# Ranks by stage for the first groups of a planned graph network kernel

## The chip, the core and the metric

The kernel runs on one core of one Trainium2 chip. The metric is the device time of one execution in microseconds (us); lower is better. A core has five engines that work side by side, each through its own instructions in a fixed order: PE (matrix products; its weight loads are shown apart as PEld), DVE and ACT (elementwise work), POOL (some small elementwise work here), and SP, which here only issues DMA transfers. They wait for each other through semaphores.

## The reference

128 graphs of 128 nodes with 256 features pass through three graph-attention layers and one gated graph network of three steps. Cut to what matters:

```python
# x [128, 128, 256], adj [128, 128, 128]
for W, a in three_layers:                    # attention layers
    h  = relu(layernorm(x))
    Wh = h @ W
    e  = leaky_relu((Wh @ a1)[:, :, None] + (Wh @ a2)[:, None, :], 0.2)
    p  = softmax(where(adj > 0, e, -9e15), axis=-1)
    x  = x + elu(p @ Wh)                     # the third layer also times nodemask
h = h0 = relu(layernorm(x))
A = adj != 0
for i in range(3):                           # gated steps
    aggr = A^T @ (h @ weight[i])
    r, z = sigmoid(aggr @ w_ih.T + h @ w_hh.T + biases)    # by halves
    n    = tanh(i_n + r * h_n)
    h    = (1 - z) * n + z * h
x = x + h
```

All of it is in 32-bit floats.

## The kernel before

**Tiling.** The graphs are cut into 33 groups: group 0 and group 32 hold 2 graphs, the others 4 (SIZES). A group g goes through seven stages: attention layers 0, 1, 2 and the normalisation behind them (`gat`, `attention`, stages l = 0 to 3), then the gated steps i = 0, 1, 2 (`gru`, `step`), and last the residual and the store (`end`).

In an attention layer, the statistics of x (st, ve, rs, nm), the normalised xn (ACT) and the scores (scr, e on DVE) are followed by a row of scores for every node. In groups 0 and 1 ("near") PE makes that row (e2, L625; the trace shows its tile as e) and PE turns the softmax weights em into at (atp, L682). In the others ("far") both go through DRAM: de and er carry the scores (L616, L618), d_at and at the turned weights. Then PE forms ahp = weights times xn (L710), ACT copies it to ah (L717), PE forms hp = ah times W (L729), and ACT and DVE add elu(hp) into x (t L743, x L745 and L747). Behind layer 2 the normalised state is hn (L778); its turned form h comes from PE (hTp, L793) in group 0 and through d_h and h in DRAM in the others, and a DVE copy (L858) puts it into the steps' layout.

A step aggregates (agp, L978; copied to ag), forms the gates' products in a recursive two by two scheme with seven products instead of eight (a, e, b from L952 and nn, nnb from L939, each for h and for ag, with DVE's sums t13 and t24 of halves), then the candidate ni (L1034), tanh, and mixes the new state. Between the steps the state is turned for the next agp: by PE (hnp, L839) in the near groups and in the last ones, through DRAM (d_hn, hn) in the others.

Before all that stands the setup: the attention vectors (`attention_weights`: ab, vp, va), the node mask (`mask`), the turned and combined weights of the gated network (`hidden`, `transposed`, `combined`: tiles whh, wih, gt, wcp, wcn, with combinations on POOL) and the biases. The steps of groups 0 and 1 wait for the whole setup (`after = last_setup`).

**What sets the order.** Nothing runs when the code above it is called: each operation is added to a `Plan` with its engine, a cost written by hand, a rank (a wish for its place; small is early) and what it reads and writes. `Plan.issue` (L108) then puts all operations in one order. Each turn it finds for each engine the operation that could start first by its costs; among those that could start within WINDOW of that one it takes the lowest rank. Operations whose rank is more than AHEAD above the lowest unfinished rank are held back. The order within each engine is fixed there, when the program is built; on the chip only the waits remain.

The ranks come from a few constants: an attention layer l of group g has rank 3g minus LEADS[g] plus 2.25 l, the normalisation behind it 5.5 instead of 2.25 l (`attention` L582, `gat` L755 and L770); step i of group g starts at BASES[g] + GAPS[g] i for the first four groups and at 3g + 2i for the others (`start`, L1167). The operations of a step have ranks near that start. The setup of the gated network has one rank, SETUP = -4.0 (L280); the attention vectors have 1.5 l - 8.0 (L299) and their loads l - 11.2. The loads of a group's x and adj have the rank of its layer 0 less 4 and less 3.6.

Of the kernel before, what the change touches and what calls it, by code (L numbers as in the profile page):

```python
# [14 lines left out]
P = 128  # L15
# [24 lines left out]
class Plan:  # L40
# [67 lines left out]
    def issue(self):  # L108
# [77 lines left out]
def kernel(  # L186
# [25 lines left out]
    nc = tc.nc  # L212
# [53 lines left out]
    def act(cols):  # L266
        return 0.25 + cols / 1400
# [70 lines left out]
    def mask():  # L338
        nm = val(su, "nm", [N], "nm")
        nmp = bank("gat", "nmp")  # L340
        load(64, SETUP, lambda: nc.sync.dma_start(nm.t[:B], nodemask), writes=[nm])
        add("PE", 0.11, SETUP, lambda: nc.tensor.transpose(nmp.t[:, :B], nm.t[:B], ident[:B, :B]),
            reads=[nm], writes=[nmp])
        add("ACT", act(P), SETUP, lambda: nc.scalar.copy(nmT.t, nmp.t[:, :B]),
            reads=[nmp], writes=[nmT])

    mask()
# [9 lines left out]
    def kept(ps, m, blocks, name):  # L357

        rz, n, raw = blocks

        def row(c):
            return ps.t.rearrange("p (g c o) -> p g c o", g=2, c=KD)[:, :, c, :]

        add("ACT", act(2 * D), SETUP, lambda: nc.scalar.mul(
            raw.t[:, m, :], ps.t, 0.5), reads=[ps], writes=[(raw, m)])
        add("ACT", act(D), SETUP, lambda: nc.scalar.mul(
            rz.t[:, m, :].rearrange("p (g o) -> p g o", g=2), row(1), 0.5,
        ), reads=[ps], writes=[(rz, m)])

    def combinations(to, raw, gates):  # L370

        def low(k):
            return raw.t[:, k, :].rearrange("p (g c o) -> p g c o", g=gates, c=KD)[:, :, 0, :]

        def of(i):
            return to.t[:, i, :].rearrange("p (g o) -> p g o", g=gates)

        def both(i, a, b, op, reads):
            return add("POOL", pool(gates * P), SETUP, lambda: nc.gpsimd.tensor_tensor(
                of(i), a(), b(), op=op), reads=reads, writes=[(to, i)])  # L380

        return [
            both(4, lambda: low(0), lambda: low(1), OP.add, [raw]),
            both(6, lambda: of(0), lambda: low(0), OP.subtract, [(to, 0), raw]),
            both(5, lambda: of(4), lambda: of(0), OP.subtract, [(to, 4), (to, 0)]),
            both(2, lambda: of(1), lambda: of(5), OP.subtract, [(to, 1), (to, 5)]),
            add("POOL", pool(gates * P), SETUP, lambda: nc.gpsimd.tensor_scalar(
                of(3), low(1), -1.0, None, op0=OP.mult), reads=[raw], writes=[(to, 3)]),
        ]

    def loaded(src, name):
        rows = src.shape[0] // P
        ld = val(su, "wld", [O3 // P, D], f"{name}_ld")
        load(128 * rows, SETUP, lambda: nc.sync.dma_start(
            ld.t[:, :rows], src.rearrange("(r p) d -> p r d", p=P)), writes=[ld])
        return ld, rows

    def turned_rows(ps, ld, k, r0, n, takes):

        def turn(r):  # L400
            add("PE", 0.11, SETUP, lambda: nc.tensor.transpose(
                ps.t[:, r * P : (r + 1) * P], ld.t[:, r0 + r, k * P : (k + 1) * P], ident
            ), reads=[ld], writes=[(ps, r)], takes=takes)

        for r in range(n):
            turn(r)

    def transposed(src, dst, name):
        ld, rows = loaded(src, name)

        def part(k, r0, n):
            ps = bank("gru", f"{name}_{k}_{r0}")
            turned_rows(ps, ld, k, r0, n, [dst])
            add("ACT", act(n * P), SETUP, lambda: nc.scalar.copy(
                dst.t[:, k, r0 * P : (r0 + n) * P], ps.t[:, : n * P]
            ), reads=[ps], writes=[(dst, (k, r0))])

# [4 lines left out]
    def hidden():  # L422
# [5 lines left out]
        def part(k):  # L428
# [5 lines left out]
            add("ACT", act(D), SETUP, lambda: nc.scalar.mul(  # L434
                raw_n.t[:, k, :], pn.t[:, :D], 0.25), reads=[pn], writes=[(raw_n, k)])
            add("ACT", act(P), SETUP, lambda: nc.scalar.mul(
                n.t[:, k, :], pn.t[:, P : 2 * P], 0.25), reads=[pn], writes=[(n, k)])

        for k in range(KD):
            part(k)  # L440
        return blocks, combinations(rz, raw, 2) + combinations(n, raw_n, 1)

    WHH, last_setup = hidden()
    wih = val(su, "wih", [KD, O3], "wih", bufs=1)
    transposed(w_ih, wih, "wih")

    def combined(i):
        gt = val(su, "gt", [KD, D], f"gt_{i}")
        transposed(gweight[i], gt, f"gt{i}")
        blocks = blocks_of(f"wc_{i}")  # L450

        def product(ps, m, o0, n):
            def one(k):
                add("PE", pe(n), SETUP, lambda: nc.tensor.matmul(
                    ps.t[:, :n], gt.t[:, k, m * P : (m + 1) * P], wih.t[:, k, o0 : o0 + n],
                    start=(k == 0), stop=(k == KD - 1),
                ), reads=[gt, wih], writes=[ps], takes=blocks)
# [4 lines left out]
        def part(m):  # L462
# [5 lines left out]
            return add("ACT", act(D), SETUP, lambda: nc.scalar.mul(  # L468
                blocks[1].t[:, m, :], pn.t[:, :D], 0.5), reads=[pn], writes=[(blocks[1], m)])

        return blocks, [part(m) for m in range(KD)] + combinations(blocks[0], blocks[2], 2)
# [2 lines left out]
    for i in range(STEPS):  # L474
        blocks, ops = combined(i)
        WC.append(blocks)
        last_setup += ops

    bi, bh, brz = (const_val(n, [NCH]) for n in ("bi", "bh", "brz"))

    def load_bias(dst, src):
        def fn():
            with nc.allow_non_contiguous_dma(reason="768 biases, once"):
                nc.sync.dma_start(dst.t, src.rearrange("(c p) -> p c", p=P))
        load(4, SETUP, fn, more=3.0, writes=[dst])

    load_bias(bi, b_ih)
    load_bias(bh, b_hh)
    add("DVE", dve(8), SETUP, lambda: nc.vector.tensor_add(brz.t, bi.t, bh.t),
        reads=[bi, bh], writes=[brz])  # L490
    add("DVE", dve(8), SETUP, lambda: nc.vector.tensor_scalar_mul(brz.t, brz.t, 0.5),
        reads=[brz], writes=[brz])
    add("DVE", dve(8), SETUP, lambda: nc.vector.tensor_scalar_mul(bh.t, bh.t, 0.5),
        reads=[bh], writes=[bh])


# [718 lines left out]
```

## Time and profile before

| | us |
|---|---|
| three runs | 2604.84, 2606.74, 2608.95 |
| median | 2606.74 |
| the profiled execution | 2606.36 |
| its span, first to last instruction | 2604.6 |
| mean granted PE clock | 0.988 of full |

The profile is of one execution. Its page gives each engine's busy time, the span in forty slices of 65 us, the chain of work that ended last, and groups of instructions. Two more views of the same trace are used: tables by stage (busy time of each engine in a stretch of time, and the clock that PE was granted in it), and the timeline (one engine's instructions in order, merged where they are alike, with the idle time before them and what ended it in brackets). A matrix product of 32-bit floats shows as two records on PE, a transpose as one. Names in the trace leave out the groups' numbers.

### The profile page before, as it was taken

What the parts mean: (1) busy time and instruction counts of PE and PEld (TensorE: products, weight loads), DVE (VectorE), ACT (ScalarE), POOL (GpSimd) and SP (SyncE); (2) the same over time, 40 slices, a digit from 0 to 9 for tenths busy, and PEclk for the clock granted to TensorE, in tenths of its full rate; (3) what the DMA queues carried; (4) which work ended last, traced back from release to release, by engine and by line L of the source; (5) the groups of instructions that cost most, each with busy time, mean ns of one, the idle gap of its engine ahead of it and who ended that gap; (6) DMA issues with size and microseconds to landing.
All of it is one profiled execution on the core that took longest, in us unless ns stands there. A gap on an engine that the chain in (4) does not pass through costs nothing.

```text
span 2604.6 us, 39011 instructions
## 1 busy us (share of the span) xinstructions
PE 2535.1 (97%) x12549; PEld 2104.6 (81%) x12549; DVE 2105.3 (81%) x4955; ACT 1768.6 (68%) x4411; POOL 225.8 (9%) x328
## 2 busy tenths in 40 slices
PE   7699799999999999999999999999999999999998
PEld 5578688788888888888888888888888888888877
DVE  6577777888888888888888888888888888888765
ACT  6566666676777676677767677766767776766554
POOL 3100000000000000000000000000000000000000
PEclk8899899999999999999999999999999999999999
DMA  3122423434334333333443434433343343333320
GB/s 92 53 54 67 108 62 101 110 101 114 94 103 108 94 108 103 112 95 98 107 104 102 114 94 105 106 97 109 103 111 93 98 112 101 94 102 85 82 63 13
DMA packets 503123, 245.75 MB, mean 94 GB/s; under 512 B 280579, under 2 KB 472067, under 8 KB 502918
## 3 DMA queue, kind: packets, MB, share of 16 engines
q1 hardware_dynamic: 502918, 243.25, 35.0%
q8 instruction: 100, 1.64, 0.3%
q14 instruction: 105, 0.86, 0.1%
HBM read 139.28 MB, written 103.87 MB: 93 GB/s over the span
## 4 chain that ended last, share of the span: by engine, by line
PE 94%; DVE 3%; ACT 2%; DMA 0%; issue 0%; SPq 0%; POOL 0%; ACTq 0%; DVEq 0%; POOLq 0%
PE b L952 19%; PE hp L729 13%; PE ni L1034 12%; PE a L952 12%; PE e L952 12%; PE ahp L710 7%; PE agp L978 6%; PE nn L939 6%; PE nnb L939 5%; DVE scr L597 0%; DVE x L745 0%; DVE st L506 0%; DVE x L747 0%; PE hnp L839 0%; ACT em L653 0%
## 5 line engine op out<-in xcount | busy, mean ns | idle before, releaser
L1034 PE MATMUL ni<-ag,wc_n 128*128 128x512 f32 (+1 forms) x792 | 353.1, 583 | 4.1 <-DVE ni L1028 4.1
L729 PE MATMUL hp<-w,ah 128*128 128x256 f32 x1536 | 355.0, 384 | 1.2 <-ACT ah L717 1.2
L729 PEld LDWEIGHTS hp<-w,ah 128*128 128x128 f32 x1536 | 285.3, 191 | 61.6 <-ACT ah L717 15.2
L597 DVE SCALAR_TENSOR_TENSOR scr<-xn,va 128x256 f32<-128x256 f32 x732 | 269.8, 417 | 35.9 <-ACT xn L589 35.5
L1034 PEld LDWEIGHTS ni<-ag,wc_n 128*128 128x128 f32 x792 | 148.5, 192 | 130.8 <-issue 105.5
L978 PEld LDWEIGHTS agp<-am,hn 128*128 128x128 f32 x1536 | 206.2, 193 | 50.6 <-issue 30.4
L743 ACT ACTIVATE t<-hp 128x512 f32<-128x512 f32 x192 | 104.8, 594 | 208.7 <-PE hp L729 208.5
L1039 ACT ACTIVATE wn<-ni,bi 128x512 f32<-128x512 f32 (+1 forms) x198 | 133.5, 674 | 151.8 <-PE ni L1034 105.3
L978 PE MATMUL agp<-am,hn 128*128 128x128 f32 x1536 | 211.8, 277 | 10.8 <-ACT hn L778 7.5
L952 PE MATMUL a<-h,whh_rz 128*128 128x256 f32 (+1 forms) x792 | 209.5, 375 | 11.2 <-DVE h L858 10.1
L710 PEld LDWEIGHTS ahp<-at,xn 128*128 128x128 f32 x1536 | 192.7, 197 | 27.1 <-issue 20.4
L512 POOL TENSOR_SCALAR ve<-st 128x4 f32<-128x4 f32 (+1 forms) x132 | 28.5, 216 | 2117.1 <-DVE st L506 1822.7
L710 PE MATMUL ahp<-at,xn 128*128 128x128 f32 x1536 | 194.4, 281 | 9.2 <-DMA at<-d_at 7.2
L589 ACT ACTIVATE xn<-x,nm,rs 128x256 f32<-128x256 f32 x366 | 201.0, 594 | 1.8 <-DVE nm L518 1.8
L952 PE MATMUL a<-ag,wc_rz 128*128 128x256 f32 (+1 forms) x792 | 200.4, 374 | 0.0
L745 DVE SCALAR_TENSOR_TENSOR x<-hp,x 128x512 f32<-128x512 f32 x192 | 124.1, 686 | 93.8 <-ACT t L743 93.6
L506 DVE BATCH_NORM_STATS2 st<-x 128x6 f32<-128x512 f32 x256 | 171.2, 690 | 2.6 <-DMA x<-in_x_dram 2.4
L636 ACT ACTIVATE em<-er,e 128x128 f32<-128x128 f32 x366 | 163.7, 522 | 6.1 <-DMA er<-de 6.1
L952 PEld LDWEIGHTS a<-h,whh_rz 128*128 128x128 f32 x792 | 141.0, 191 | 27.2 <-DVE h L858 10.6
L653 ACT ACTIVATE em<-em,nmx 128x128 f32<-128x128 f32 x384 | 149.5, 392 | 11.3 <-DVE nmx L649 11.0
L952 PEld LDWEIGHTS a<-ag,wc_rz 128*128 128x128 f32 x792 | 141.1, 191 | 15.1 <-issue 0.5
L717 ACT COPY ah<-ahp 128x512 f32<-128x512 f32 (+1 forms) x198 | 113.3, 573 | 56.8 <-PE ahp L710 50.6
(158 smaller groups left out, 5574.2 us busy)
## 6 DMA issues: line engine op xcount, KB each, us to landing
d_hn<-tr_hn SPq DMA_DIRECT2D x116, 256.0 KB, 2.4
hn<-d_hn SPq DMA_DIRECT2D x464, 64.0 KB, 2.3
er<-de SPq DMA_DIRECT2D x90, 256.0 KB, 3.9
d_at<-tr_at SPq DMA_DIRECT2D x90, 256.0 KB, 2.0
at<-d_at SPq DMA_DIRECT2D x360, 64.0 KB, 2.1
x<-in_x_dram SPq DMA_DIRECT2D x31, 512.0 KB, 5.1
d_h<-tr_h SPq DMA_DIRECT2D x31, 512.0 KB, 2.8
h<-d_h SPq DMA_DIRECT2D x124, 128.0 KB, 2.8
```

Of the source, the lines that this page charges most:

```text
L506: add("DVE", dve(T), rank, lambda: nc.vector.bn_stats(st.t[:, b, :].rearrange("p b s -> p (b s)"), xt.t[:, b, :].rearrange("p b d -> p d b ...
L589: add("ACT", 0.45, rank, lambda: nc.scalar.activation(xn.t[:, b, :], xt.t[:, b, :], AF.Relu, bias=nm.t[:, b : b + 1], scale=rs.t[:, b : b ...
L597: add("DVE", dve(D), rank, lambda: nc.vector.scalar_tensor_tensor(scr.t, xn.t[:, b, :], 1.0 if far else rs.t[:, b : b + 1], VA[l].t[:, s, ...
L636: add("ACT", 0.55 if far else 0.42, rank, lambda: nc.scalar.activation(em.t[:, b, :], e2_row(b), AF.Prelu, bias=e.t[:, 0, b : b + 1], alph ...
L653: add("ACT", 0.42, rank, lambda: nc.scalar.activation(em.t[:, b, :], em.t[:, b, :], AF.Exp, bias=nmx.t[:, b : b + 1], accum_out=sm.t[:, b ...
L710: add("PE", pe(P), rank, lambda: nc.tensor.matmul(summed(ps, b), xn.t[:, b, k * P : (k + 1) * P], turned_weights(b), start=True, stop=True ...
L729: add("PE", pe(D), rank, lambda: nc.tensor.matmul(hp.t[:, b * D : (b + 1) * D], ah.t[:, k, c * P : (c + 1) * P], W[l].t[:, k, :], start=(k ...
L939: op = add("PE", pe(H), at, lambda: nc.tensor.matmul(ps.t[:, o : o + H], WHH[1].t[:, blk, :], rhs(), start=starts, stop=True, skip_group_c ...
L952: nc.tensor.matmul(ps.t[:, gate * D : gate * D + H], w[0].t[:, blk, gate * P : (gate + 1) * P], rhs(), start=go, stop=w is not WHH, skip_g ...
L978: nc.tensor.matmul(ps.t[:, b * P : (b + 1) * P], s, am.t[:, b, :], start=True, stop=True)
L1034: add("PE", pe(TG), rank + 0.45 + 0.05 * c, lambda k=k: nc.tensor.matmul(ni[c].t[:, :TG], WC[i][1].t[:, k, c * P : (c + 1) * P], ag.t[:, k ...
L1039: add("ACT", act(TG) + 0.05, quick, lambda: nc.scalar.activation(wn[c].t[:, :TG], ni[c].t[:, :TG], AF.Tanh, bias=bi.t[:, cn : cn + 1]), re ...
```

## The change

Only ranks and the constants that govern their use change; wherever an operation of the setup had SETUP, it now has setup_rank().

1. In the plan, WINDOW goes from 0.1 to 0.097 and AHEAD from 3.5 to 4.12; while the lowest unfinished rank is at most UNTIL = -1.46, EARLY = 5.0 stands for AHEAD.
2. The setup's one rank becomes a list by piece: the mask -4.77 instead of -4.0, all other pieces -3.63.
3. The attention vectors of the three layers get -6.42, -7.21, -4.35 instead of -8.0, -6.5, -5.0; their loads -11.17, -10.17, -7.80 instead of -11.2, -10.2, -9.2.
4. The first ten groups' ranks come from a table with a number for each stage (ATT) instead of a number for each group, and the steps' starts of the first eight groups from another (STARTS). Later groups keep the formula. Group 3's attention, for example, goes from 2.0, 4.25, 6.5, 7.5 to -0.38, 1.67, 4.29, 4.81; group 2's from -4.5, -2.25, 0, 1 to -3.70, -1.92, 1.59, 3.59; group 1's from -6.0, -3.75, -1.5, -0.5 to -7.16, -4.64, -3.85, -2.65; group 0's first step from 0 to 1.68.

```diff
-    WINDOW = 0.1
-    AHEAD = 3.5
+    WINDOW = 0.097
+    AHEAD = 4.12
+    EARLY = 5.00
+    UNTIL = -1.46
...
-            limit = by_rank[low].rank + self.AHEAD
+            limit = by_rank[low].rank
+            limit += self.AHEAD if limit > self.UNTIL else self.EARLY
...
-    SETUP = -4.0
+    SETUPS = [-4.77, -3.63, -3.63, -3.63, -3.63, -3.63, -3.63]
+    setting = [0]
+
+    def setup_rank():
+
+        return SETUPS[setting[0]]
...
-        rank = 1.5 * l - 8.0
+        rank = [-6.42, -7.21, -4.35][l]
...
-        first = l - 11.2
+        first = [-11.17, -10.17, -7.80][l]
...
+    setting[0] = 1
     WHH, last_setup = hidden()
+    setting[0] = 2
     wih = val(su, "wih", [KD, O3], "wih", bufs=1)
     transposed(w_ih, wih, "wih")
 
     def combined(i):
+        setting[0] = 3 + i
...
-        rank = 3.0 * g - lead(g) + SPAN * l
+        rank = stage(g, l)
...
-        rank = 3.0 * g - lead(g)
+        rank = stage(g, 0)
...
-        rank = 3.0 * g - lead(g) + HEAD
+        rank = stage(g, 3)
...
-    BASES = [0.00, 3.00, 6.00, 9.00]
-    GAPS = [2.00, 2.00, 2.25, 2.00]
...
-    LEADS = [7.50, 9.00, 10.50, 7.00, 7.75, 7.25, 8.50, 8.50, 8.50, 8.50]
...
+    ATT = [
+        [-8.90, -4.73, -3.23, -1.30],
+        [-7.16, -4.64, -3.85, -2.65],
+        [-3.70, -1.92, 1.59, 3.59],
+        [-0.38, 1.67, 4.29, 4.81],
+        [3.81, 5.72, 6.93, 8.03],
+        [7.96, 10.27, 13.26, 12.41],
+        [9.50, 11.75, 14.74, 15.00],
+        [12.46, 14.80, 17.00, 18.00],
+        [15.66, 17.97, 20.00, 21.29],
+        [18.50, 20.75, 23.00, 24.00],
+    ]
+    STARTS = [
+        [1.68, 2.28, 4.42],
+        [3.03, 4.63, 6.47],
+        [5.97, 6.79, 10.50],
+        [9.00, 11.18, 12.82],
+        [12.28, 14.00, 16.00],
+        [14.67, 16.85, 19.17],
+        [17.30, 19.87, 22.34],
+        [21.00, 23.00, 25.06],
+    ]
+
+    def stage(g, l):
+
+        return ATT[g][l] if g < len(ATT) else 3.0 * g - LEAD + (SPAN * l if l < 3 else HEAD)
 
     def start(g, i):
 
-        return BASES[g] + GAPS[g] * i if g < len(BASES) else 3.0 * g + 2.0 * i
+        return STARTS[g][i] if g < len(STARTS) else 3.0 * g + 2.0 * i
```

More of the change, by code (lines that the diff above doesn't have):

```diff
@@ L340, in mask @@
         nmp = bank("gat", "nmp")
-        load(64, SETUP, lambda: nc.sync.dma_start(nm.t[:B], nodemask), writes=[nm])
-        add("PE", 0.11, SETUP, lambda: nc.tensor.transpose(nmp.t[:, :B], nm.t[:B], ident[:B, :B]),
+        load(64, setup_rank(), lambda: nc.sync.dma_start(nm.t[:B], nodemask), writes=[nm])
+        add("PE", 0.11, setup_rank(), lambda: nc.tensor.transpose(nmp.t[:, :B], nm.t[:B], ident[:B, :B]),
             reads=[nm], writes=[nmp])
-        add("ACT", act(P), SETUP, lambda: nc.scalar.copy(nmT.t, nmp.t[:, :B]),
+        add("ACT", act(P), setup_rank(), lambda: nc.scalar.copy(nmT.t, nmp.t[:, :B]),
             reads=[nmp], writes=[nmT])
@@ L362, in row @@
             return ps.t.rearrange("p (g c o) -> p g c o", g=2, c=KD)[:, :, c, :]
-        add("ACT", act(2 * D), SETUP, lambda: nc.scalar.mul(
+        add("ACT", act(2 * D), setup_rank(), lambda: nc.scalar.mul(
             raw.t[:, m, :], ps.t, 0.5), reads=[ps], writes=[(raw, m)])
-        add("ACT", act(D), SETUP, lambda: nc.scalar.mul(
+        add("ACT", act(D), setup_rank(), lambda: nc.scalar.mul(
             rz.t[:, m, :].rearrange("p (g o) -> p g o", g=2), row(1), 0.5,
@@ L378, in both @@
         def both(i, a, b, op, reads):
-            return add("POOL", pool(gates * P), SETUP, lambda: nc.gpsimd.tensor_tensor(
+            return add("POOL", pool(gates * P), setup_rank(), lambda: nc.gpsimd.tensor_tensor(
                 of(i), a(), b(), op=op), reads=reads, writes=[(to, i)])
@@ L386, in combinations @@
             both(2, lambda: of(1), lambda: of(5), OP.subtract, [(to, 1), (to, 5)]),
-            add("POOL", pool(gates * P), SETUP, lambda: nc.gpsimd.tensor_scalar(
+            add("POOL", pool(gates * P), setup_rank(), lambda: nc.gpsimd.tensor_scalar(
                 of(3), low(1), -1.0, None, op0=OP.mult), reads=[raw], writes=[(to, 3)]),
@@ L393, in loaded @@
         ld = val(su, "wld", [O3 // P, D], f"{name}_ld")
-        load(128 * rows, SETUP, lambda: nc.sync.dma_start(
+        load(128 * rows, setup_rank(), lambda: nc.sync.dma_start(
             ld.t[:, :rows], src.rearrange("(r p) d -> p r d", p=P)), writes=[ld])
@@ L400, in turn @@
         def turn(r):
-            add("PE", 0.11, SETUP, lambda: nc.tensor.transpose(
+            add("PE", 0.11, setup_rank(), lambda: nc.tensor.transpose(
                 ps.t[:, r * P : (r + 1) * P], ld.t[:, r0 + r, k * P : (k + 1) * P], ident
@@ L413, in part @@
             turned_rows(ps, ld, k, r0, n, [dst])
-            add("ACT", act(n * P), SETUP, lambda: nc.scalar.copy(
+            add("ACT", act(n * P), setup_rank(), lambda: nc.scalar.copy(
                 dst.t[:, k, r0 * P : (r0 + n) * P], ps.t[:, : n * P]
@@ L433, in part @@
             turned_rows(pn, ld, k, 4, 2, [*blocks, raw_n])
-            add("ACT", act(D), SETUP, lambda: nc.scalar.mul(
+            add("ACT", act(D), setup_rank(), lambda: nc.scalar.mul(
                 raw_n.t[:, k, :], pn.t[:, :D], 0.25), reads=[pn], writes=[(raw_n, k)])
-            add("ACT", act(P), SETUP, lambda: nc.scalar.mul(
+            add("ACT", act(P), setup_rank(), lambda: nc.scalar.mul(
                 n.t[:, k, :], pn.t[:, P : 2 * P], 0.25), reads=[pn], writes=[(n, k)])
@@ L453, in one @@
             def one(k):
-                add("PE", pe(n), SETUP, lambda: nc.tensor.matmul(
+                add("PE", pe(n), setup_rank(), lambda: nc.tensor.matmul(
                     ps.t[:, :n], gt.t[:, k, m * P : (m + 1) * P], wih.t[:, k, o0 : o0 + n],
@@ L467, in part @@
             product(pn, m, 2 * D, D)
-            return add("ACT", act(D), SETUP, lambda: nc.scalar.mul(
+            return add("ACT", act(D), setup_rank(), lambda: nc.scalar.mul(
                 blocks[1].t[:, m, :], pn.t[:, :D], 0.5), reads=[pn], writes=[(blocks[1], m)])
@@ L477 @@
         last_setup += ops
+    setting[0] = 6
     bi, bh, brz = (const_val(n, [NCH]) for n in ("bi", "bh", "brz"))
@@ L484, in fn @@
                 nc.sync.dma_start(dst.t, src.rearrange("(c p) -> p c", p=P))
-        load(4, SETUP, fn, more=3.0, writes=[dst])
+        load(4, setup_rank(), fn, more=3.0, writes=[dst])
     load_bias(bi, b_ih)
     load_bias(bh, b_hh)
-    add("DVE", dve(8), SETUP, lambda: nc.vector.tensor_add(brz.t, bi.t, bh.t),
+    add("DVE", dve(8), setup_rank(), lambda: nc.vector.tensor_add(brz.t, bi.t, bh.t),
         reads=[bi, bh], writes=[brz])
-    add("DVE", dve(8), SETUP, lambda: nc.vector.tensor_scalar_mul(brz.t, brz.t, 0.5),
+    add("DVE", dve(8), setup_rank(), lambda: nc.vector.tensor_scalar_mul(brz.t, brz.t, 0.5),
         reads=[brz], writes=[brz])
-    add("DVE", dve(8), SETUP, lambda: nc.vector.tensor_scalar_mul(bh.t, bh.t, 0.5),
+    add("DVE", dve(8), setup_rank(), lambda: nc.vector.tensor_scalar_mul(bh.t, bh.t, 0.5),
         reads=[bh], writes=[bh])
@@ L1148, in gru @@
         return step, end
-    URGENT = 1.0
-    BASES = [0.00, 3.00, 6.00, 9.00]
-    GAPS = [2.00, 2.00, 2.25, 2.00]
+    URGENT = 1.00
     SPAN = 2.25
@@ L1160 @@
     LEAD = 8.5
-    LEADS = [7.50, 9.00, 10.50, 7.00, 7.75, 7.25, 8.50, 8.50, 8.50, 8.50]
-    def lead(g):
-        return LEADS[g] if g < len(LEADS) else LEAD
+    ATT = [
[22 more added lines that the diff above has]
+        return ATT[g][l] if g < len(ATT) else 3.0 * g - LEAD + (SPAN * l if l < 3 else HEAD)
     def start(g, i):
-        return BASES[g] + GAPS[g] * i if g < len(BASES) else 3.0 * g + 2.0 * i
+        return STARTS[g][i] if g < len(STARTS) else 3.0 * g + 2.0 * i
     work, h = {}, {}
```

## The prediction

> **What bounds the kernel now.** I read the page first: its busy shares, the forty slices, the chain that ended last.
>
> ```profile
> PE 2535.1 (97%) x12549; PEld 2104.6 (81%) x12549; DVE 2105.3 (81%) x4955; ACT 1768.6 (68%) x4411; POOL 225.8 (9%) x328
> ...
> PE   7699799999999999999999999999999999999998
> ...
> PEclk8899899999999999999999999999999999999999
> ...
> PE 94%; DVE 3%; ACT 2%; DMA 0%; issue 0%; SPq 0%; POOL 0%; ACTq 0%; DVEq 0%; POOLq 0%
> ```
>
> PE is full except in slices of the first 340 us, and there its clock is short as well. So the kernel has two regimes, and a new order can win only where PE has holes. The table by stage (columns: stretch, its length, busy time of PE, weight loads, DVE, ACT, POOL with counts, clock, DMA share, GB/s) says how much:
>
> ```profile
> 0.00:40.00 40.00, 32.16 (x140) 23.26 (x141) 25.82 (x91) 25.19 (x72) 10.00 (x22) 0.83 0.50 150
> 40.00:140.00 100.00, 69.60 (x331) 54.04 (x330) 54.90 (x156) 56.59 (x162) 22.45 (x31) 0.85 0.12 35
> 140.00:200.00 60.00, 56.84 (x349) 49.23 (x349) 48.49 (x140) 43.78 (x118) 7.97 (x11) 1.00 0.24 62
> 200.00:300.00 100.00, 98.61 (x491) 82.48 (x491) 77.14 (x187) 69.55 (x173) 5.72 (x8) 1.00 0.28 77
> 300.00:340.00 40.00, 25.12 (x106) 20.47 (x105) 29.16 (x76) 23.50 (x61) 4.20 (x7) 0.79 0.37 94
> 480.00:500.00 20.00, 16.09 (x77) 13.77 (x76) 15.72 (x43) 9.07 (x26) 1.86 (x4) 1.00 0.46 110
> 604.00:2500.00 1896.00, 1895.57 (x9309) 1578.25 (x9308) 1596.13 (x3684) 1319.07 (x3257) 152.62 (x217) 1.00 0.38 101
> ```
>
> From 604 to 2500 us PE idles 0.43 us: nothing is to be had. From 40 to 140 us no engine is full (PE 70%, DVE 55%, ACT 57%): serial chains bound it. PE's timeline shows the holes and who ended them:
>
> ```profile
> 62.89 0.47 PE L682 MATMUL atp<-ident,em 128*128 128x128 f32 x1 [5.54 <-ACT em L666]
> 84.56 0.47 PE L625 MATMUL e<-ident,e 128*128 128x128 f32 x1 [5.72 <-DVE scr L597]
> 117.23 3.65 PE L1034 MATMUL ni<-ag,wc_n 128*128 128x256 f32 x8 [3.31 <-DVE ni L1028]
> 128.09 3.75 PE L710 MATMUL ahp<-at,xn 128*128 128x128 f32 x16 [7.21 <-DMA at<-d_at]
> 310.40 2.27 PE L978 MATMUL agp<-am,hn 128*128 128x128 f32 x8 [7.48 <-ACT hn L778]
> 322.15 2.08 PE L952 MATMUL a<-h,whh_rz 128*128 128x256 f32 x4 [6.72 <-DVE h L858]
> 476.94 1.05 PE L978 MATMUL agp<-am,hn 128*128 128x128 f32 x8
> 487.56 1.13 PE L952 MATMUL a<-h,whh_rz 128*128 128x256 f32 x4 [3.37 <-DVE h L858]
> ```
>
> Now a measure that holds idle time and slow clock together. In the dense stretch a PE product (two records) follows the last after 0.223 us (128 columns), 0.432 (256) or 0.858 (512), a transpose after 0.11. Over all PE instructions that is 2493 us of full-clock work. "Lag" is time minus the full-clock work done by then; what a new order wins is lag. Before: 18 us at 40, 45 at 98 (group 0's first aggregation), 52 at 121 (its first GRU step done), 59 at 128, 70 at 200, 72 at 300, 90 at 322, 93 at 480, 97 at 500, 101 at 2520, 107.5 at PE's last instruction.
>
> **What the Trainium skill says.** "TensorE: Matmul & The Clock Gate", Part 1: an idle window of about 3.4 us halves PE's clock until it has been busy for about as long. The trace agrees: the granted clock from 309 to 323 us is 0.50, and the eight aggregation records take 2.27 us at 310 against 1.05 at 477. So the 14.9 us idle from 300 to 322 cost 17.6 us of lag. "Perfetto Trace Analysis", Optimization Strategy: regimes with different limits gain from being interleaved; the stage table shows two such. "DMA: Bandwidth & Descriptors", Latency and other measured facts: about 2 us fixed cost per transfer; the page's issues land in a median 2.0 to 2.8 us, and one turned state (out and back) is two of them.
>
> **The change part by part.** It adds and removes no instruction: in the built programs each engine has the same ones (6349 products and transposes on PE, 1659 DMAs on SP). Only the order differs, and only early: PE's is identical from the instruction that ran at 604 us, POOL's from 312, DVE's, ACT's and SP's from 762. So the tail costs as before, and AHEAD 4.12 and WINDOW 0.097 do nothing in the steady part. All that counts is the lag on entering the common order: 97 before. I count in the new order how much full-clock PE work ("cover") lies between a producer and its consumer on PE, and hold it against how long that hand-over took in the trace.
>
> *Start to group 0's first aggregation.* The long chain is group 1's three layers. Before, all products of the weights' setup (wcp and wcn, 12 of 0.858 and 12 of 0.432, 15.5 us) stood ahead of the second half of its layer 1's e2 rows, which ran at 56.8; the 5.5 us hole follows. Now two of the 24 do, and those rows end at 29 us of PE work instead of 38. The chain by the trace: hp of layer 0 done at 36; to e2 8.5 (36.5 to 45.0) plus 2 to issue; to atp 5.7; to ahp 1.9; ahp and ah 2.4, hp 3.5: 60. Layer 2: 9.9 to e2 (the 84.56 wait ended it), then 0.5, 5.7, 1.9, 2.4, 3.5: 84. Group 0's hTp follows its hp by 8.1, at about 86; group 2's ahp and hp take 5: first aggregation at 91 with 58.4 us of work done, lag 32 against 45. DVE and ACT bound this from the other side: the new order brings group 3's first layer in here, so at the end of group 0's first step they have done 81.5 and 80.9 us against 74.9 and 76.9. From 40 us DVE owes 55.7; at 55% (as now) that ends at 141, at 81% (as from 140 to 200) at 109. I take 77%: the step ends at 112 with 68.9 us of PE work, lag 43 against 52, keeping 36 (86%) and 61 (62%) for the range. A step needs 13 us (agp at 138.6 to ni at 151.5), so by the chain alone it ends at 107.
>
> *To 139 us of work.* The 7.21 us wait: cover from group 2's hp to its next ahp goes from 16.1 to 27.4, against 31.6 us that hand-over took; shortfall at most 4, mostly eaten by gaps in between. Interleaved with the steps of groups 0 and 1 remain short waits on agp and b (seven of 0.5 to 0.7 us from 138 to 184 before). +7: lag 50 against 70.
>
> *Groups 1 to 3.* Before +2 to 300 us; I take +3, since covers of 2.7 and 4.8 us before group 1's hnp are near the 3 us of tanh and mix (rows of 0.69). The hole of 17.6: cover from group 3's last hp to its agp goes from 3.4 to 48.1. Gone. Group 2's same hand-over shrinks from 37 to 21.5, but there what counts is its turned state: 11.9 us of work from its transpose to the h copy, against 9.2 (313.2 to 322.4) and 11.2 (476.6 to 487.8) measured. +0.5.
>
> *To the common order.* +3 to 480 as before. The 487.56 wait, 4.5 us of lag: group 5's normalised state is transposed 7.3 us of work after its hp instead of 13.4, leaving 11.4 for the turn that took 11.2. Group 4's state between steps 1 and 2 has only 9.5 us of cover instead of 23.9; such a turn took 11.8 without a wait at group 2. +2.5 for both (0 to 9).
>
> Sum: 43 + 7 + 3 + 0.5 + 3 + 2.5 = 59, against 97.3: 38 us less. POOL's and SP's reordering I cost at nothing: the combinations on POOL end by 44 us of work, 25 ahead of the first step's end, and x and adj of groups 4 to 9 are loaded 80 us of work or more before use. If that cover failed, a step would show a DMA wait. The profiled execution took 2606.36 (span 2604.6 and 1.8 around it), 0.4 below the median 2606.74: forecast 2568.
>
> **The rivals.**
> - Denser packing (17%). DVE and ACT reach 86% early, as DVE's 95% from 140 to 160 suggests they can: lag 36 + 5 + 2 + 3 = 46, 51 us less, 2555. Against: each engine takes its queue in the plan's order, and the near layers are serial.
> - The vector engines become the early bound (14%). At 62% the first step ends at 130, lag 61 + 16 = 77, 20 us less, 2586. For: the ranks now put group 3's exchanges among the near groups' chains.
> - New holes in the middle (13%): groups 2, 4, 5 with covers of 21.5, 9.5, 19.5 each miss by 4 us, with slow clock after them 12 more: 2580.
> - Slower (3%). A blocked head of a queue: ACT's first read of er for group 3 (em L636), put between group 0's and group 1's work at 62 us of PE work, waits for its DMA, and both chains behind it. Before, ACT idled 6.1 us for er in all. It decides only above 38 us of it; with 43, 2612.
> - The order makes no difference to the time (3%): it would need the holes to reappear one for one; 2606.
>
> Mine has 50%.
>
> **How the numbers follow.** The likeliest is 2568. Range 2553 to 2587: all of mine and of the new holes, most of the two packing rivals. Over and under 0.2% (5 us, what a measurement here can tell): faster 0.94, same 0.03, slower 0.03.
>
> **What would show it.** Right: the stretch 300 to 340 at clock 1.00 with PE full; no wait on hn L778; group 0's first agp near 91 to 97 and DVE above 70% from 40 to 110; PE without idle from about 460 on. Wrong: ACT or DVE idle on er in the first 110 us, DVE at 55% there still, or new waits on h L858 or on hn for groups 2, 4 and 5.

## The result, and the profile after

| | us |
|---|---|
| before, four runs beside it | 2604.84 to 2608.95, median 2607.84 |
| after, four runs | 2566.03 to 2569.20, median 2566.86 |
| ratio | 0.9846, 95% interval 0.9829 to 0.9863 |
| the profiled execution of after | 2566.74, its span 2565.0, mean PE clock 0.993 |

The changed kernel is 1.5% faster, 41 us by the medians. Its code stands 9 to 13 lines lower: L710 (ahp) is now L723, L729 (hp) L742, L952 (a, e, b) L965, L978 (agp) L991, L597 (scores) L610.

First the page of the profile of after: busy shares, PE's forty slices and granted clock, the chain that ended last.

```profile
PE 2527.7 (99%) x12549; PEld 2098.6 (82%) x12549; DVE 2105.9 (82%) x4955; ACT 1768.5 (69%) x4411; POOL 225.1 (9%) x328
...
PE   8799999999999999999999999999999999999998
...
PEclk8899999999999999999999999999999999999999
...
PE 95%; DVE 2%; ACT 2%; DMA 1%; issue 0%; SPq 0%; POOL 0%; ACTq 0%; DVEq 0%
```

The instruction counts are those of before. The fifth slice (260 to 325 us), a 7 before with a clock of 8, is full at full clock. The table by stage of after, with the columns of the table of before:

```profile
40.00:140.00 100.00, 81.67 (x449) 65.34 (x449) 74.27 (x219) 72.79 (x210) 24.86 (x35) 0.93 0.16 46
140.00:200.00 60.00, 58.76 (x331) 50.93 (x330) 48.39 (x129) 47.22 (x125) 6.93 (x9) 1.00 0.19 61
300.00:340.00 40.00, 39.73 (x191) 32.26 (x190) 33.32 (x85) 29.12 (x69) 4.29 (x5) 1.00 0.39 99
480.00:500.00 20.00, 20.00 (x102) 17.12 (x101) 13.92 (x33) 16.23 (x48) 2.25 (x3) 1.00 0.43 118
```

From 40 to 140 us PE now does 449 instructions instead of 331, with DVE at 74% and ACT at 73% instead of 55% and 57%: more work is done beside the serial chains. From 300 to 340 PE does 191 instead of 106. PE's timeline of after, the waits that are left:

```profile
72.20 0.32 PE L638 MATMUL e<-ident,e 128*128 128x128 f32 x1 [1.08 <-DVE scr L610]
...
80.97 1.11 PE L695 MATMUL atp<-ident,em 128*128 128x128 f32 x4 [3.37 <-ACT ah L730]
...
95.13 2.02 PE L723 MATMUL ahp<-at,xn 128*128 128x128 f32 x16 [1.97 <-DMA at<-d_at]
...
105.18 0.71 PE L991 MATMUL agp<-am,hn 128*128 128x128 f32 x4 [2.27 <-ACT ag L999]
...
136.06 1.95 PE L723 MATMUL ahp<-at,xn 128*128 128x128 f32 x16
...
452.50 1.13 PE L965 MATMUL e<-t13h,whh_rz 128*128 128x256 f32 x4 [0.43 <-DVE t13h L929]
```

The largest idle time in these lines is 3.37 us; before had 5.5, 5.7, 7.2, 7.5 and 6.7. Group 2's products that waited 7.21 us for the transfer of at start at 136.06 without a gap. The wait of 3.37 at 487 us is gone; around 450 us PE now waits four times, for 0.28 to 0.68.

By the prediction's lag (time minus full-clock PE work done), in us:

| at | before | predicted | after |
|---|---|---|---|
| group 0's first aggregation | 45 | 32 | 42.5 |
| end of its first step | 52 | 43 | 47.3 |
| 139 us of work | 70 | 50 | 52.8 |
| 300 us of work | 91.7 | 53.5 | 54.5 |
| entry into the common order | 97.3 | 59 | 57.9 |
| PE's last instruction | 107.5 | 69 | 68.0 |

From the entry on both kernels lose the same 10 us.

### The profile page after: what moved, and what is told of

It is laid out like the page before. It is cut to its first block, busy times and chain, and to the rows that moved or that the text cites. A ratio compares the mean times of both kernels' runs of the same rounds, so it can differ in the third digit from the quotient of the medians.

```text
span 2565.0 us, 39018 instructions
## 1 busy us (share of the span) xinstructions
PE 2527.7 (99%) x12549; PEld 2098.6 (82%) x12549; DVE 2105.9 (82%) x4955; ACT 1768.5 (69%) x4411; POOL 225.1 (9%) x328
## 4 chain that ended last, share of the span: by engine, by line
PE 95%; DVE 2%; ACT 2%; DMA 1%; issue 0%; SPq 0%; POOL 0%; ACTq 0%; DVEq 0%
PE b L965 19%; PE hp L742 13%; PE e L965 13%; PE ni L1047 13%; PE a L965 13%; PE ahp L723 7%; PE agp L991 6%; PE nn L952 6%; PE nnb L952 5%; ACT em L666 0%; DVE scr L610 0%; ACT em L679 0%; PE hnp L852 0%; DMA at<-d_at 0%; ACT hn L791 0%
## 5 line engine op out<-in xcount | busy, mean ns | idle before, releaser
L742 PE MATMUL hp<-w,ah 128*128 128x256 f32 x1536 | 356.2, 384 | 0.5 <-ACT ah L730 0.5
L742 PEld LDWEIGHTS hp<-w,ah 128*128 128x128 f32 x1536 | 286.7, 191 | 61.9 <-ACT ah L730 13.1
L610 DVE SCALAR_TENSOR_TENSOR scr<-xn,va 128x256 f32<-128x256 f32 x732 | 270.3, 418 | 36.1 <-ACT xn L602 35.8
L991 PEld LDWEIGHTS agp<-am,hn 128*128 128x128 f32 x1536 | 204.7, 191 | 42.7 <-issue 30.8
L991 PE MATMUL agp<-am,hn 128*128 128x128 f32 x1536 | 208.9, 275 | 3.6 <-ACT ag L999 3.0
L965 PE MATMUL a<-h,whh_rz 128*128 128x256 f32 (+1 forms) x792 | 208.8, 373 | 0.8 <-ACT z L1035 0.5
L723 PEld LDWEIGHTS ahp<-at,xn 128*128 128x128 f32 x1536 | 190.6, 196 | 23.0 <-issue 14.4
L965 PE MATMUL a<-ag,wc_rz 128*128 128x256 f32 (+1 forms) x792 | 199.1, 373 | 0.0
L723 PE MATMUL ahp<-at,xn 128*128 128x128 f32 x1536 | 192.5, 279 | 4.6 <-DMA at<-d_at 2.8
L666 ACT ACTIVATE em<-em,nmx 128x128 f32<-128x128 f32 x384 | 149.4, 392 | 11.6 <-DVE nmx L662 11.4
L965 PEld LDWEIGHTS a<-h,whh_rz 128*128 128x128 f32 x792 | 140.9, 191 | 16.9 <-issue 0.7
L965 PEld LDWEIGHTS a<-ag,wc_rz 128*128 128x128 f32 x792 | 141.1, 191 | 15.2 <-issue 0.5
L528 POOL TENSOR_TENSOR rs<-ve,mhalf 128x4 f32<-128x4 f32 (+1 forms) x132 | 144.0, 1091 | 11.0
```

Of the source, the lines that this page charges most:

```text
L528: add("POOL", 1.04, rank, lambda: nc.gpsimd.tensor_tensor(rs.t, ve.t, mhalf[:, :n], op=OP.pow), reads=[ve], writes=[rs])
L610: add("DVE", dve(D), rank, lambda: nc.vector.scalar_tensor_tensor(scr.t, xn.t[:, b, :], 1.0 if far else rs.t[:, b : b + 1], VA[l].t[:, s, ...
L666: add("ACT", 0.42, rank, lambda: nc.scalar.activation(em.t[:, b, :], em.t[:, b, :], AF.Exp, bias=nmx.t[:, b : b + 1], accum_out=sm.t[:, b ...
L723: add("PE", pe(P), rank, lambda: nc.tensor.matmul(summed(ps, b), xn.t[:, b, k * P : (k + 1) * P], turned_weights(b), start=True, stop=True ...
L742: add("PE", pe(D), rank, lambda: nc.tensor.matmul(hp.t[:, b * D : (b + 1) * D], ah.t[:, k, c * P : (c + 1) * P], W[l].t[:, k, :], start=(k ...
L965: nc.tensor.matmul(ps.t[:, gate * D : gate * D + H], w[0].t[:, blk, gate * P : (gate + 1) * P], rhs(), start=go, stop=w is not WHH, skip_g ...
```

## The experiments

Two theories stood first. A, the prediction's: each hole comes and goes with the PE work that lies between producer and consumer, so it can be said in advance where undoing a part brings one back. B: the parts add up, each worth a share of the 41 us. A third, E, came out of the first eight runs; C and D are about what still delays the early chain.

### One part alone, from the kernel before

t_setup: only the list of the setup's ranks, and the attention vectors' ranks and loads.

```diff
-    SETUP = -4.0
+    SETUPS = [-4.77, -3.63, -3.63, -3.63, -3.63, -3.63, -3.63]
...
-        rank = 1.5 * l - 8.0
+        rank = [-6.42, -7.21, -4.35][l]
...
-        first = l - 11.2
+        first = [-11.17, -10.17, -7.80][l]
```

> The kernel before with only the setup's and the attention vectors' new ranks. PE's order differs only up to 67 us of PE work. Theory A (holes by cover: PE waits where the work between producer and consumer is less than the hand-over takes): group 1's e2 rows of layer 1 end at 24.5 us of work instead of 37.8, so the 5.5 us hole goes; but group 2's cover from hp to its next ahp falls from 16.1 to 10.4 us against 31.6, so most of it is given back there; the holes at 310 and 487 stay: about 2601. Theory B (the gain is made by packing the first 100 us, and the parts add up): what is won by group 0's first aggregation stays, some 14 us: 2592.

t_plan: only the plan's constants.

```diff
-    WINDOW = 0.1
-    AHEAD = 3.5
+    WINDOW = 0.097
+    AHEAD = 4.12
+    EARLY = 5.00
+    UNTIL = -1.46
...
-            limit = by_rank[low].rank + self.AHEAD
+            limit = by_rank[low].rank
+            limit += self.AHEAD if limit > self.UNTIL else self.EARLY
```

> The kernel before with only the plan's constants (WINDOW 0.097, AHEAD 4.12, EARLY 5.0 up to UNTIL). Theory A: group 3's turned state still has 0.7 us of work between its transpose and its use, so the 17.6 us of lag at 310 stay; group 2's ahp has 21.2 us of cover instead of 16.1, worth up to 5: 2600 to 2607. Theory B: more operations open to the plan in the first part fill the idle PE there, some 10 us: 2596.

t_tables: only the two tables, ATT and STARTS.

```diff
-        rank = 3.0 * g - lead(g) + SPAN * l
+        rank = stage(g, l)
...
-        return BASES[g] + GAPS[g] * i if g < len(BASES) else 3.0 * g + 2.0 * i
+        return STARTS[g][i] if g < len(STARTS) else 3.0 * g + 2.0 * i
```

> The kernel before with only the two tables (ATT and STARTS). Theory A: the holes at 310 and 487 go (22 us of lag; covers from transpose to use are 44.7 and 10.5 us of work), but group 2's cover from hp to ahp falls to 5.2 us, so a wait of over 10 us stays there, and group 3's turn after step 0 has 7.3 us against some 10: 2590. Theory B: the tables are most of the change and bring most of the 41 us: 2575.

t_g3: of the tables only the row of group 3's attention.

```diff
+    def stage(g, l):
+
+        if g == 3:
+            return [-0.38, 1.67, 4.29, 4.81][l]
+        return 3.0 * g - lead(g) + (SPAN * l if l < 3 else HEAD)
```

> The kernel before with only the four attention ranks of group 3 from the table. Theory A: the hole of 17.6 us of lag at 310 goes (28.8 us of work between transpose and use), group 5's at 487 grows by some 4 us (4.8 us of work instead of 8.7): 2593. Theory B: group 3 lies outside the first 100 us, so little changes: 2604.

Measured, with the kernel before at a median of 2608.52 beside them; lag in us at so much PE work done, and in the last column what a later group's period of 76.8 us of work adds to the lag (mean of twelve, from 1268 to 2190 us of work). The lag is that of the profiled execution, which for t_g3 was the longest of its four (2640.38):

| | median us | ratio (95% interval) | 70 | 140 | 240 | 500 | 2300 | a period |
|---|---|---|---|---|---|---|---|---|
| before | 2608.52 | | 60.6 | 69.8 | 91.3 | 97.4 | 100.9 | 0.12 |
| t_setup | 2622.58 | 1.0058 (1.0043 to 1.0073) | 76.7 | 85.2 | 107.9 | 114.7 | 118.1 | 0.12 |
| t_plan | 2624.76 | 1.0065 (1.0050 to 1.0080) | 56.4 | 66.7 | 95.9 | 115.9 | 119.8 | 0.12 |
| t_tables | 2641.62 | 1.0128 (1.0111 to 1.0145) | 76.6 | 89.2 | 90.7 | 101.0 | 135.6 | 1.07 |
| t_g3 | 2634.48 | 1.0106 (1.0087 to 1.0125) | 67.7 | 84.2 | 84.7 | 101.8 | 133.2 | 1.09 |

B falls: the three parts that make up the change are each slower than before, by 14, 16 and 33 us, and together 41 faster. A holds for most places and fails for the sizes: its four numbers were too low by 18 to 52 us. In t_g3 the hole of group 3 is gone as A says: 0.5 us of lag from 140 to 240 us of work, against 21.5 before. But it is paid for ahead of it (14 us more at 140). t_plan keeps that hole, as A says, and opens waits that A did not have (5.41 us at 259 us, before an e of group 1's third step). What is late there in t_setup and t_tables is the turn of the far groups' weights through DRAM. PE's timeline of t_setup, in which the setup stands later and more near work ahead of it:

```profile
105.87 3.76 PE L719 MATMUL ahp<-at,xn 128*128 128x128 f32 x16 [4.11 <-DMA at<-d_at]
...
144.36 3.76 PE L719 MATMUL ahp<-at,xn 128*128 128x128 f32 x16 [10.74 <-DMA at<-d_at]
```

and of t_tables, where the tables alone move the far groups. By the built order this wait stands before group 3's first layer; before group 2's second, where A had put one of over 10 us, 2.66 are left:

```profile
128.08 3.39 PE L710 MATMUL ahp<-at,xn 128*128 128x128 f32 x16 [20.12 <-DMA at<-d_at]
```

The clock pays for each such hole a second time: the sixteen records behind each hole of t_setup took 3.76 us at a granted clock of 0.50, those of after at 136.06 took 1.95 at 1.00. And the last column has what neither theory had: two of the four lose 1.1 us, on average, in each later period.

### One part undone, from the kernel after

a_g3back: group 3's row as before.

```diff
-        [-0.38, 1.67, 4.29, 4.81],
+        [2.00, 4.25, 6.50, 7.50],
```

> The kernel after with group 3's four attention ranks of before. Theory A: the hole at group 3's first step comes back (no work at all between its last hp and its agp, 5.3 us between transpose and use), 17 to 22 us of lag, and group 5's too (2.2 us of work against 11: 9 us): 2595. Theory B (DVE and ACT bound the first part): with group 3's first layer out of it, DVE and ACT owe 4.3 and 5.6 us less at the end of group 0's first step, which comes that much earlier: 2563 to 2570.

a_setupback: the setup and the attention vectors as before.

```diff
-    SETUPS = [-4.77, -3.63, -3.63, -3.63, -3.63, -3.63, -3.63]
+    SETUPS = [-4.0] * 7
...
-        rank = [-6.42, -7.21, -4.35][l]
+        rank = 1.5 * l - 8.0
...
-        first = [-11.17, -10.17, -7.80][l]
+        first = l - 11.2
```

> The kernel after with the setup's and attention vectors' ranks of before. Theory A: group 5's last hp now stands directly before its agp (no work between, 0.9 us between transpose and use), so a hole of some 20 us opens there; the early part loses a little: 2588. Theory B: only the early part suffers, as DVE owes 86.7 instead of 81.1 us at the end of group 0's first step: 2575.

a_planback: the plan's constants as before.

```diff
-    WINDOW = 0.097
-    AHEAD = 4.12
-    EARLY = 5.00
+    WINDOW = 0.1
+    AHEAD = 3.5
+    EARLY = 3.5
```

> The kernel after with the plan's constants of before (WINDOW 0.1, AHEAD 3.5 throughout). Theory A: group 2's cover from hp to ahp is 5.2 us instead of 27.4, a wait of 10 to 20 us, and group 5's turned state has 2.2 us, 9 more: 2590. Theory B: the constants open work early and the loss lies in the first 100 us, some 10: 2577.

a_noearly: only the wider opening in the first part is taken away.

```diff
-    UNTIL = -1.46
+    UNTIL = -99.0
```

> The kernel after with AHEAD 4.12 throughout, no EARLY. Theory A: group 2's cover from hp to ahp is 15.7 us, worth a wait of some 8, and group 5's turned state has 0.9 us of work, worth 10: 2585. Theory B: only the first part changes, by the 5.7 us more that DVE owes by group 0's first step: 2573.

Measured (before 2607.82 beside them):

| | median us | ratio to before (95% interval) | 70 | 140 | 240 | 500 | 2300 | a period |
|---|---|---|---|---|---|---|---|---|
| after | 2566.86 | 0.9846 (0.9829 to 0.9863) | 48.4 | 52.8 | 53.7 | 57.9 | 61.3 | 0.12 |
| a_g3back | 2639.54 | 1.0128 (1.0113 to 1.0143) | 44.5 | 52.4 | 71.8 | 96.8 | 131.6 | 1.47 |
| a_setupback | 2635.49 | 1.0106 (1.0090 to 1.0123) | 62.6 | 80.7 | 82.7 | 110.2 | 134.0 | see below |
| a_planback | 2679.17 | 1.0275 (1.0260 to 1.0291) | 91.9 | 103.4 | 107.8 | 136.9 | 171.9 | 1.47 |
| a_noearly | 2656.61 | 1.0192 (1.0177 to 1.0207) | 67.7 | 81.3 | 82.1 | 112.0 | 148.6 | 1.48 |

Every one of these parts is needed: take any one away, and the kernel is slower than before. (The two tables as a whole were not taken out of after.) Both theories' numbers were too low again, A's by 45 to 89 us and B's by more. a_g3back brings the hole back where A put it. PE's timeline of a_g3back:

```profile
293.35 1.29 PE L991 MATMUL agp<-am,hn 128*128 128x128 f32 x4 [7.88 <-ACT hn L791]
...
301.99 3.75 PE L723 MATMUL ahp<-at,xn 128*128 128x128 f32 x16 [2.45 <-DMA at<-d_at]
...
468.43 3.75 PE L723 MATMUL ahp<-at,xn 128*128 128x128 f32 x16 [5.19 <-DMA at<-d_at]
...
484.73 2.08 PE L965 MATMUL a<-h,whh_rz 128*128 128x256 f32 x4 [5.85 <-DVE h L871]
```

It costs 19.4 us of lag from 140 to 240 us of work (52.4 to 71.8), after 0.9: the same hole that cost 17.6 before. Group 3's early row itself costs 3.9 us at 70 us of work (48.4 against 44.5), made up by 140.

That is one of three stretches in which these kernels lose. From 240 to 500 us of work all four lose 25 to 30 us, after 4.2. A had put a hole at group 5's turned state there in each of the four, and each has it: PE waits 4.8 to 6.1 us before the same a (the last line above). In a_g3back shorter waits stand ahead of it, the longest on the turned weights of group 7's first layer (the line at 468.43). From 500 to 2300 they lose 24 to 37 us, after 3.4: the subject of the next section.

At 70 us of work the ranks of the setup and the attention vectors are worth 14 us, the early opening 19, the plan's constants together 43; these don't add up, since each is measured with the others in place. In a_planback four long waits stand before that point: 9.1 us for the normalised state of group 0, and by the built order 6.3, 13.9 and 10.8 for the turned weights of groups 2, 3 and 2 again. PE's timeline of a_planback has the last two:

```profile
134.00 3.76 PE L723 MATMUL ahp<-at,xn 128*128 128x128 f32 x16 [13.93 <-DMA at<-d_at]
...
152.56 3.76 PE L723 MATMUL ahp<-at,xn 128*128 128x128 f32 x16 [10.84 <-DMA at<-d_at]
```

A had forecast the last of the four, 10 to 20 us, and not the others. Its counts point the way of the difference: the plan's new constants raise group 2's cover from 5.2 to 27.4 us of work with the tables and the new setup in place, and only from 16.1 to 21.2 without them, where they are worth 4 us at 70 (60.6 to 56.4).

### A second price: the steady part

Four kernels (before, after, t_setup, t_plan) lose 0.12 us a period and six others (a_startsback below among them) 1.1 to 1.5. The built programs show who belongs where: PE's order becomes that of before for good after 506 us of work in after, 67 in t_setup and 558 in t_plan; in the six it differs until about 2400. a_setupback reaches it at about 1095, and its lag, grown to 131.5 by then, adds 2.5 more in the rest. PE's timeline in the steady part, first of after:

```profile
1086.99 0.59 PE L952 MATMUL nn<-t13h,whh_n 128*128 128x256 f32 x2
1087.43 1.95 PE L723 MATMUL ahp<-at,xn 128*128 128x128 f32 x16
1089.21 0.60 PE L965 MATMUL b<-t24h,whh_rz 128*128 128x256 f32 x2
```

then of a_g3back:

```profile
1114.87 0.59 PE L952 MATMUL nn<-t13h,whh_n 128*128 128x256 f32 x2
1115.83 1.13 PE L965 MATMUL b<-t24h,whh_rz 128*128 128x256 f32 x4 [0.36 <-ACT b L1099]
```

In after another group's ahp lies between a step's nn and its b; in a_g3back b follows at once and waits for ACT's copy out of the bank it needs. Such places are short and many. The same 619.2 us by engine (the columns of the table by stage), first after, then a_g3back:

```profile
1100.00:1719.20 619.20, 619.20 (x3047) 516.44 (x3046) 525.97 (x1224) 437.34 (x1086) 51.12 (x73) 1.00 0.38 103
```

```profile
1100.00:1719.20 619.20, 615.27 (x2997) 503.38 (x2996) 515.15 (x1205) 433.02 (x1065) 48.25 (x71) 1.00 0.38 102
```

PE shows 0.6% idle and does 1.6% fewer instructions. The distance from one start to the next, against its full-clock value, finds the rest: over eight periods 11.6 us too much in a_g3back and about 1 in after, the largest share (4.2) from nn to b, no single gap over 0.54. This is one pattern for four of the six: by the records a_g3back, a_planback and a_noearly have the same PE order from 736 to 2146 us of work, and a_startsback has it from 1448. t_tables and t_g3 have others, with gaps that were not taken apart.

From this came theory E: a change of early ranks has two separate prices, the lag until the tables end and the pattern that the plan then falls into. a_startsback tests it: after with the steps' starts of before.

```diff
     STARTS = [
-        [1.68, 2.28, 4.42],
-        [3.03, 4.63, 6.47],
-        [5.97, 6.79, 10.50],
-        [9.00, 11.18, 12.82],
-        [12.28, 14.00, 16.00],
-        [14.67, 16.85, 19.17],
-        [17.30, 19.87, 22.34],
-        [21.00, 23.00, 25.06],
+        [0.00, 2.00, 4.00],
+        [3.00, 5.00, 7.00],
+        [6.00, 8.25, 10.50],
+        [9.00, 11.00, 13.00],
     ]
```

> The kernel after with only the steps' starts of before. Theory E (whether the order falls into the steady pattern that before and after share decides over some 34 us; the eight runs above showed it): in the built program PE's order never joins that pattern before the last groups, so 1.45 us are lost in each of some 24 periods, and group 5's turned state has 7.4 us of work against 11: 2567 + 34 + 5 = 2606. Rival A (only the early holes count): 2575.

Measured: 2621.39 (2620.06 to 2623.29), ratio to before 1.0054 (1.0041 to 1.0066). The lag is 47.9 at 70 us of work, 80.7 at 500 and 115.8 at 2300: the growth of 35 in the steady part is E's 34. By the total E misses by 15 and A alone by 46. The early part E had too small: 22.8 us more lag than after at 500, where E had 5. Of that, 15 come between 70 and 140 us of work, where PE's longest wait is 6.11 us before an nnb of group 1's first step, and 6 between 240 and 500.

### What still delays the early chain

The first aggregation came at 101 instead of 91. Beside group 1's layer 2 the timeline shows scores (scr, DVE) of twice the usual length, with combinations of weights running on POOL. DVE's timeline of after:

```profile
69.81 0.93 DVE L610 SCALAR_TENSOR_TENSOR scr<-xn,rs,va 128x256 f32<-128x256 f32 x1
...
70.67 0.93 DVE L610 SCALAR_TENSOR_TENSOR scr<-xn,rs,va 128x256 f32<-128x256 f32 x1
```

POOL's timeline of after at the same time:

```profile
69.55 0.91 POOL L388 TENSOR_TENSOR wc_rz<-wc_raw 128x256 f32<-128x256 f32 x1
70.42 0.90 POOL L388 TENSOR_TENSOR wc_rz<-wc_rz,wc_raw 128x256 f32<-128x256 f32 x1
71.30 1.02 POOL L396 TENSOR_SCALAR wc_rz<-wc_raw 128x256 f32<-128x256 f32 x1
```

The two keep pace: each of these two scores starts 0.25 us behind a POOL instruction and takes 0.45 us longer than alone. "SBUF — State Buffer" in the Trainium skill says, under "SBUF: two separate sides", that DVE and GpSimd (POOL) share one pair of ports as an exclusive lock, and that a DVE instruction with two inputs in SBUF and a POOL instruction that reads SBUF block each other for a whole instruction. This trace agrees that they hinder each other, and not for how long: one after the other, a score and a combination would take 0.48 + 0.72 = 1.20 us, and here a pair takes 0.87. Theory C: without that overlap the chain is shorter. Theory D: what C wins is lost again at the next wait, the 3.37 us for ACT's copy ah, since the bank that atp needs comes free only after other work in ACT's queue. Two kernels test this. a_portfree makes the ten combinations of the second and third combined weights short. It clears the rest of those blocks with one early operation on DVE, and so leaves out part of the weights of two steps; it shows what the overlap costs and is no version to use:

```diff
+        w = 4 if setting[0] > 3 else P
...
-                of(i), a(), b(), op=op), reads=reads, writes=[(to, i)])
+                of(i)[:, :, :w], a()[:, :, :w], b()[:, :, :w], op=op), reads=reads, writes=[(to, i)])
```

> The kernel after with the ten POOL combinations of the second and third combined weights cut to 4 of each 128 columns (the rest of those blocks stays zero, so two steps compute with part of their weights left out). Order on every engine as after. In the trace of after, six score operations of group 1's layer 2 take 0.93 us instead of 0.48 where a POOL combination runs beside them. Theory C (DVE and POOL hinder each other at the memory, on the longest chain): all twelve-odd near scores take 0.48, e2 of group 1's layer 2 ends some 3.5 us earlier, group 0's first aggregation starts 3 us earlier, and the lag on entering the common order falls by 2 to 3: 2564. Rival D (the chain through group 2's far layer or ACT's queue decides there): the scores are faster, the first aggregation isn't: 2567.

a_held keeps them whole, but holds them in POOL's queue behind a small POOL operation that reads group 1's last scores:

```diff
+        order = [op for op in order if op not in self.held_back]
+        at = order.index(self.release) + 1
+        order[at:at] = self.held_back
...
+        if (g, l) == (1, 2):
+            seen = val(su, "seen", [2], "seen", bufs=1)
+            plan.release = add("POOL", 0.01, rank, lambda: nc.gpsimd.tensor_scalar(
+                seen.t, e.t[:, :, n - 1], 1.0, None, op0=OP.mult),
+                reads=[(e, (s, n - 1)) for s in range(2)], writes=[seen])
```

> The kernel after with those ten POOL combinations whole but held back in POOL's queue behind a small POOL operation that reads group 1's last scores of layer 2; order on the other engines as after. Theory C: the scores are free of POOL, but the combinations then run beside em and the next statistics, so that about half of the gain is left: 2565. If POOL's combinations now delay group 0's last statistics (ve L525) it is lost: 2567 to 2569. Rival D: 2567.

after_again is after unchanged.

> The kernel after once more, beside the next ones: 2567, its trace with the same holes.

Measured (before 2608.28 beside them):

| | median us (range) | ratio to before (95% interval) | group 1's layer 1, end of hp, to layer 2's atp, us | from the same hp to group 0's first aggregation, us |
|---|---|---|---|---|
| after, its first four runs (before 2607.84) | 2566.86 (2566.03 to 2569.20) | 0.9846 (0.9829 to 0.9863) | 19.2 | 39.2 |
| after_again | 2569.16 (2567.77 to 2570.99) | 0.9853 (0.9840 to 0.9867) | 19.2 | 41.5 |
| a_portfree | 2565.96 (2564.53 to 2566.11) | 0.9838 (0.9825 to 0.9852) | 16.1 | 37.7 |
| a_held | 2565.11 (2561.51 to 2569.53) | 0.9838 (0.9824 to 0.9852) | 16.5 | 37.8 |

DVE's timeline of a_portfree, the scores of the same layer:

```profile
68.15 0.48 DVE L615 SCALAR_TENSOR_TENSOR scr<-xn,rs,va 128x256 f32<-128x256 f32 x1
```

C's mechanism is shown: all eight scores take 0.48 to 0.51 in both kernels, where six of eight took about 0.93 in after, and the chain is 3 us shorter up to atp. D is there too: the wait before that atp grows from 3.37 to 4.28 and 4.73 us. Up to the first aggregation the gain is 1.5 to 3.8 us, by which of the two traces of after it is held against, and whether it reaches the end is not settled: by the medians a_held is 0.16% faster than after_again and 0.07% faster than the first runs of after, and the intervals overlap. No version here is shown to beat after.

## Why the prediction came out

The forecast was 2568, the measured median 2566.86. By its own steps:

- **Only the early order counts; the tail costs as before.** Right: 97.3 became 57.9 at the entry, 39.4 less, and the end is 39.5 earlier (107.5 to 68.0). This step carried more than the prediction said of it. It rested on finding the same PE order in both built programs; in the kernels where that did not hold, the lag grew by 24 to 37 us from 500 to 2300 us of work, instead of about 3.5.
- **Start to the first aggregation, lag 32.** Wrong by 10.5 us (42.5): the mis-sized term. The chain was the right one, and it slipped by 1.4 to 2.8 us at each link: layer 1's hp ended at 61.8 (60 predicted), layer 2's e2 at 73.9 (70.5), its atp came at 81.0 (76), hp ended at 91.7 (84), the aggregation came at 101.0 (91, so its sign "near 91 to 97" failed). The durations were taken from a trace in which that layer's scores ran undisturbed (0.47 to 0.48); the new order put POOL's combinations beside them, worth some 3 us up to atp by a_portfree and a_held. The rest is other work in the queues, which the prediction counted as fixed hand-overs: atp waited 3.37 for ACT's ah copy, six records of group 0's hp then stood ahead of group 1's ahp on PE for 2.77 (81.88 to 84.65, at a granted clock of 0.50), and group 2's ahp waited 1.97 for its at. "POOL's and SP's reordering I cost at nothing" was wrong for POOL: the combinations were early enough for their readers and in the way of a neighbour.
- **DVE's 77%, the first step's end at lag 43.** DVE did 74% from 40 to 110 us and 59% before. The step ended at 47.3, 5 after its aggregation instead of 11: the second term was too long by 6.
- **To 139 us of work, +7.** It was +5.5 (47.3 to 52.8); of the 7.21 us wait nothing is left.
- **Groups 1 to 3, +3.5, and the hole of 17.6 gone.** Right: +1.7 from 139 to 300 us of work, hn's wait is gone, the clock from 300 to 340 is 1.00. a_g3back put the row back and got 19.4 us back. That this row closes the hole is shown, by t_g3 from the other side too.
- **To the common order, +3 and +2.5.** It was +3.4 for both: the four waits around 450 us take 1.7 us together.
- **The rivals.** No wait of ACT on er shows in the first 110 us, and the new holes on h or hn in the middle did not come: from 300 us on PE's longest wait before the common order is 0.68. Denser packing (lag 46) and the vector engines as the bound (77) both miss.

So the total of 59 against 57.9 is in part luck: the first term was 10.5 us short and the four behind it 6.2, 1.5, 1.8 and 2.1 long, 11.6 in all. Two readings are off, and no term of the sum uses them: 2.0 to 2.8 us is the landing time of turned states and weights only (er and x of before took 3.9 and 5.1), and the rows that were to end at 29 us of PE work, the second half of group 1's layer 1, end at 23.7 in the trace of after. The mechanism (holes close where other PE work is put between producer and consumer) is shown by t_g3, a_g3back and the two traces.

Open: what in the plan's turn decides which steady pattern it falls into, and why the losses came out so much larger than A's covers gave; neither was tried further.

## What to carry to other kernels

In a kernel whose order is fixed when it is built, compare the built orders first. Here, where PE's order became the same for good, the kernels lost the same from there on; where it didn't, a change of early ranks cost some 30 us in the steady part, through gaps of about half a microsecond and less. Price a moved operation not only by whether its readers still get it in time, but by what runs beside it in its new place. Parts of such a tuning need not be separate gains: here each alone lost 14 to 33 us, so a part that fails alone says little about the whole.

## What the runs showed that was not expected

A score with a scale per row (scr<-xn,rs,va on DVE) took 0.93 us beside a combination on POOL and 0.48 without, while POOL's went from 0.72 to 0.90. The far groups' scores (scr<-xn,va) read two tiles of the same kinds, with a constant for the scale, and take 0.42 alone. In twelve profiled runs (before, after and ten of the experiments, without a_portfree and a_held) these scores lay beside a combination for 0.3 us or more 87 times:

| | beside a combination with two inputs (L388 of after) | beside the one with one input (L396) |
|---|---|---|
| scale per row | 62 of 64 took 0.65 to 1.05, most 0.93 to 0.97 | 17 took 0.50 to 0.62 |
| constant scale | 2 took 0.94 | 4 took 0.41 |

The two exceptions, 0.47 and 0.48, had started 0.10 and 0.06 us before their combination, and there POOL's took 0.97 and 1.02. DVE's timeline of after has one of the four,

```profile
66.08 0.41 DVE L610 SCALAR_TENSOR_TENSOR scr<-xn,va 128x256 f32<-128x256 f32 x1
```

and POOL's timeline of after what ran beside it:

```profile
65.75 0.85 POOL L396 TENSOR_SCALAR wc_rz<-wc_raw 128x256 f32<-128x256 f32 x1
```

So the records divide by POOL's instruction: beside two inputs the scores are about twice as long whatever their scale, beside one input a score with a constant scale is not longer at all, although that instruction reads SBUF too. No kernel varied this by itself, and the constant scale has only six cases.

Also, four profiled runs whose PE order is the same (after, after_again, a_portfree, a_held) reached 20 us of PE work with lags of 21.2, 19.3, 21.2 and 22.9. At 2300 us of work they stood at 61.3, 63.5, 60.5 and 63.8. So runs with one PE order differ by 2 to 4 us, and the start alone does not say which ends later.
